# Attention steps taken in twos: where the values' product and the other work stand between the scores

## The chip, the cores and the metric

The kernel runs on one core of one Trainium2 chip. The metric is the device time of one execution in microseconds (us); lower is better. Each core has five engines with queues of their own: TensorE (PE, matrix products and transposes; its weight loads are shown as PEld), VectorE (DVE), ScalarE (ACT), GpSimd (POOL) and SyncE (SP, which issues DMAs). Each engine works through its queue in the order in which the program was written and waits at semaphores for the others. Matrix products are written to PSUM, from where DVE or ACT read them.

## The reference

`x` is (8, 512, 256) in f32. Four residual blocks follow each other, each on a layer norm of what came before:

```
x = x + attn_a(layernorm(x))     # 16 heads of 16, latent kv, RoPE, relative decay, softmax, plus a gated memory term
x = x + ffn(layernorm(x))        # 256 -> 1024 -> 256, relu
x = x + attn_b(layernorm(x))     # (q k^T * causal decay) v, no softmax
x = x + ffn(layernorm(x))        # the same weights again
```

The change concerns `attn_a`. Per head it is

```
att = softmax(q k^T / 4 + log_sparse + log(decay))    # 512 x 512 per head
out = att v + 0.2 * sigmoid(q . mean(k)) * mean(v)
```

The kernel computes the softmax as exp(0.25 * (score - row maximum)) times a table (`dec_a`, the exponential of the two added terms), and divides by the row sum after the product with v (v has a column of ones for that).

## The kernel before

Attention is cut into 32 groups (8 batch entries times 4 groups of 4 heads), each into 8 items: 4 tiles of 128 rows times 2 pairs of heads, so 256 items in all. An item passes four stations:

- *Scores s* (`score_item`, `reduce_item`): two products of 128 x 512 (32 rows of the array each) into one PSUM tile of two banks; DVE reads it once for the row maximum (`mr`).
- *Shift*: when all 8 items of a group have their maxima, one transpose (`mx`), one ACT instruction (`neg`) and a DMA put the negated maxima into spare rows of qT.
- *Transposed scores t* (`prob_item`, `soft_item`): k against q with the shift included, again two products into one PSUM tile; ACT takes the exponential into a tile `p` in SBUF; then the *decay*, two multiplications of 128 x 512 by `dec_a`, on DVE or, for every third item (`on_pool`), on POOL.
- *Values* (`pv_item`): for two items together, 4 products that add into the group's one PSUM tile `pv`, each on 32 columns of the array.

The scores s and t share the pool `ps_sc` with two buffers (four PSUM banks); `pv` has one bank, all other products (`ps_m`) three. So all eight banks are used. `p` has four buffers.

The order of all engines' instructions is written out by a planner in Python at build time. A *step* t (`step`) holds the scores of item t, the transposed scores of item t - 10 (`LAG`), and in every second step the values of items t - 12 and t - 13. Everything else (layer norms, projections, RoPE, both feed-forward blocks, `attn_b`, the output product) is cut into *units* with an assumed TensorE time and follow-up times for the other engines, in one chain for each batch entry's front part and one for its rest. The main loop (lines 898 to 945) asks for the earliest start of the next step (`step_start`) and of the best unit (`start_of`), and issues units while a credit lasts; each step adds to the credit the share of the remaining unit work that falls to one step. Below, a *run* of other work is what stands between two blocks of scores or values on TensorE. The clocks in this planner are assumptions; on the chip only queues and semaphores count.

In a step the order was: values' product first (if it has one), then s and t, then on ACT and DVE the exponential, the maximum and the decay; units follow until the next step. Items below `EARLY` = 34 use tiles of `ps_m` for t instead; they are done by step 43.

Of the kernel before, what the change touches and what calls it, by code (L numbers as in the profile page):

```python
# [35 lines left out]
def tile_kernel(  # L36
# [210 lines left out]
    NS = 8 * NI  # L247
    LAG, PVLAG = 10, 2
    PER = 8 * NG
    EARLY = PER + 2  # L250
# [249 lines left out]
    probs, pv = {}, {}  # L500

    def on_pool(n):
        return n % 2 == 0 if n < EARLY else n % 3 == 2
# [20 lines left out]
    def soft_item(n, ps):  # L524
        i, r = divmod(n, 8)
        t, pair = r // 2, 1 - r % 2
        p = at.tile([P, 2, T], F32, tag="p", bufs=4, name=f"p_{n}")
        if n < EARLY:
            for e in range(2):
                act.activation(p[:, e, :], ps[e], AF.Exp, scale=0.25)  # L530
        else:
            act.activation(p, ps[2], AF.Exp, scale=0.25)
        o = (NT - 1 - t) * P
        eng = gps if on_pool(n) else dve
        for e in range(2):
            eng.tensor_tensor(p[:, e, :], p[:, e, :], late["dec_a"][:, o : o + T], ALU.mult)
        probs[(i, t, pair)] = p

    def pv_item(n):
        i, r = divmod(n, 8)  # L540
        t = r // 2
        if t == 0:
            pv[i] = ps_pv.tile([P, T], F32, tag="pv", name=f"pv_{i}")
        g, va = i % NG, vaug[(i // NG) % 2]
        for h in range(4):
            mm(
                pv[i][h * 32 : h * 32 + 32, :], va[:, t, (NG * g + h) * 17 : (NG * g + h) * 17 + 32], probs[(i, t, h // 2)][:, h % 2, :],
                t == 0, t == NT - 1,
            )
        probs.pop((i, t, 0)), probs.pop((i, t, 1))  # L550
# [4 lines left out]
    def post_units(i):  # L555
        b, g = divmod(i, NG)
        s = {}

        def evacuate():
            num = at.tile([P, T], F32, tag="num", name=f"num_{i}")  # L560
            act.copy(num, pv[i])
            s["num"] = num

        def divide():
            if g == 0:
                a_tok[b] = at.tile([P, NT, D], F32, tag="atok", bufs=1, name=f"atok_{b}")
                aT[b] = at.tile([P, NC, T], F32, tag="aT", name=f"aT_{b}")
            ps = misc(f"num_{i}")
            for t in range(NT):
                flip(ps[:, t * P : (t + 1) * P], s["num"][:, t * P : (t + 1) * P])  # L570
            pn = ps.rearrange("p (t h d) -> p t h d", h=4, d=32)
            rd = at.tile([P, NT, 4], F32, tag="rd", name=f"rd_{i}")
            dve.reciprocal(rd, pn[:, :, :, HD])
            dve.tensor_tensor(
                a_tok[b][:, :, g * 64 : (g + 1) * 64].rearrange("p t (h d) -> p t h d", d=HD),
                pn[:, :, :, :HD], rd.unsqueeze(3).to_broadcast([P, NT, 4, HD]), ALU.mult,
            )

        def turn():
            c = g // 2  # L580
            ps = misc(f"aT_{i}")
            for t in range(NT):
                flip(ps[:, t * P : (t + 1) * P], a_tok[b][:, t, c * P : (c + 1) * P])
            act.copy(aT[b][:, c, :], ps)

        u = [Unit(evacuate, then=(("ACT", 600),))]
        u.append(Unit(divide, 520, (("DVE", 700),), after=u[-1:]))
        if g % 2:
            u.append(Unit(turn, 520, (("ACT", 600),), after=u[-1:], gives=("aT", b) if g == NG - 1 else None))
        return u  # L590
# [165 lines left out]
    clock = {"PE": 0, "DVE": 0, "ACT": 0, "POOL": 0}  # L756
    banks = deque([0, 0, 0])
# [52 lines left out]
    def values_of(t):  # L810
        n = steps[t][2]
        return n if n > 0 and n % 2 == 1 else None

    def step_start(t):

        s, ts, _ = steps[t]
        n = values_of(t)
        at_ = clock["PE"]
        if n is not None:
            at_ = max(at_, prob_at[n] - 100, prob_at[n - 1] - 100)  # L820
        own = 0
        need = (s is not None) + sum(i >= EARLY for i in ts)
        if need:
            own = sc[need - 1]
        for i in ts:
            if i < EARLY:
                own = max(own, banks[1])
            if shifted[i // 8].done is None:
                return None
            own = max(own, shifted[i // 8].done + 2300)  # L830
        return max(at_, own - (1000 if n is not None else 0))

    def step(t):
        s, ts, _ = steps[t]
        at_ = step_start(t)
        n = values_of(t)
        if n is not None:
            pv_item(n)
            at_ += 1000
            if n % 8 == 7:  # L840
                us = post_units(n // 8)
                made = Unit(None)
                made.done = at_ + 100
                us[0].after.append(made)
                posts.extend(us)
        mms, after = [], []
        if s is not None:
            ps, m = score_item(s)
            mms += m
            after.append((reduce_item, s, ps))  # L850
        for i in ts:
            ps, m = prob_item(i)
            mms += m
            after.append((soft_item, i, ps))
        for o, l, r in mms:
            mm(o, l, r)
        if mms:
            at_ += 1080
        clock["PE"] = at_
        for f, k, ps in after:  # L860
            f(k, ps)
        if s is not None:
            maxed[s] = clock["DVE"] = max(clock["DVE"], at_ + 100) + 1280
            sc.popleft()
            sc.append(maxed[s])
            if s % 8 == 7:
                posts.append(shift_unit(s // 8))
        for i in ts:
            if i < EARLY:
                for e in range(2):  # L870
                    clock["ACT"] = max(clock["ACT"], at_ + 100) + 650
                    banks.popleft()
                    banks.append(clock["ACT"])
            else:
                clock["ACT"] = max(clock["ACT"], at_ + 100) + 1090
                sc.popleft()
                sc.append(clock["ACT"])
            e = "POOL" if on_pool(i) else "DVE"
            prob_at[i] = clock[e] = max(clock[e], clock["ACT"] + 60) + (2700 if on_pool(i) else 1500)

    posts = []
    setup = [Unit(lambda: fetch(2), step=20)]
# [16 lines left out]
    while t < LAST or any(chains) or posts:  # L899
        while True:  # L900
            ready = [
                c for c in [posts] + chains
                if c and not c[0].pe and c[0].step <= t and start_of(c[0]) is not None
                and start_of(c[0]) <= clock["PE"] + 300
            ]
            if not ready:
                break
            for c in ready:
                issue(c.pop(0))
        best = None  # L910
        for rank, c in enumerate([posts] + chains):
            if not c or not c[0].pe or c[0].step > t:
                continue
            s = start_of(c[0])
            if s is None:
                continue
            key = (max(s, clock["PE"] + 50), rank)
            if best is None or key < best[0]:
                best = (key, c, s)
        s_step = step_start(t) if t < LAST else None  # L920
        if t < LAST:
            take = best is not None and (best[1] is posts or credit > 0) and (
                s_step is None or best[2] <= max(clock["PE"] + 50, s_step)
            )
            take = take or (best is not None and s_step is not None and best[2] + best[1][0].pe <= s_step)
            take = take or (best is not None and s_step is None)
            if not take and s_step is None:
                raise AssertionError("nothing to do")
        else:
            take = True  # L930
        if take and best is None:

            c = min((c for c in [posts] + chains if c and start_of(c[0]) is not None), key=lambda c: start_of(c[0]))
            clock["PE"] = max(clock["PE"], start_of(c[0]))
            issue(c.pop(0))
        elif take:
            if best[1] is not posts:
                credit -= best[1][0].pe
            issue(best[1].pop(0))
        else:  # L940
            step(t)
            t += 1
            left = sum(u.pe for c in chains for u in c) - tail_work
            share = max(0, left) / max(1, LAST - t)
            credit = min(credit, share) + share


# [107 lines left out]
```

## Time and profile before

| what | value |
|---|---|
| median of 3 runs | 1343.89 us (1341.66 to 1344.9) |
| profiled execution, its own time | 1341.52 us |
| its span, first to last instruction | 1339.7 us |
| mean granted TensorE clock | 0.978 |
| PE busy | 1256.3 us, 94% of the span |
| DVE busy | 811.0 us, 61% |
| ACT busy | 450.0 us, 34% |
| POOL busy | 405.8 us, 30% |

How to read the lines below: a line of a group names the line of the source (L69 and L205 are helpers that record every instruction), the engine, the operation, output<-inputs, shapes and count, then busy time and mean duration in ns, then the idle time of the engine before these instructions and what ended it. A line of the waits says who waited for whom, with the total in us, the count and the longest. A line of the timeline gives start, duration (both us), engine, instruction, and in brackets the idle time before it and its releaser; several records of one kind are merged into one line (xcount). Each f32 product appears as two records, a transpose as one. Matmuls are pipelined, so neighbouring ones overlap in the records; the distance from start to start is what counts.

### The profile page before, as it was taken

How to read it: one execution, taken by the hardware profiler on the slowest of the kernel's cores; microseconds unless marked ns; L12 is line 12 of the kernel's file. 1: busy time of each engine (PE TensorE's matmuls, PEld its weight loads, DVE VectorE, ACT ScalarE, POOL GpSimd, SP SyncE). 2: the span in 40 equal slices, each digit the busy share in tenths (PEclk: the TensorE clock that was granted, in tenths of full speed). 3: DMA queues.
4: the chain of work that ended last, by engine and by line, in shares of the span. 5: the costliest groups of instructions: out<-in, count | busy, mean ns of one | idle time of the engine just before them, and what ended most of it. 6: DMA issues, size and time to landing. Idle time of an engine off the chain costs nothing. (4 is left out here: it accounts for less than half of the span.)

```text
span 1339.7 us, 15533 instructions
## 1 busy us (share of the span) xinstructions
PE 1256.3 (94%) x6116; PEld 623.3 (47%) x6116; DVE 811.0 (61%) x1323; ACT 450.0 (34%) x646; POOL 405.8 (30%) x461
## 2 busy tenths in 40 slices
PE   6899888999899999999999999999999899999988
PEld 3333232534354455453443554544444445455665
DVE  4588885667656774657856666657755575343130
ACT  2044434333434334433334334333333333321201
POOL 4165542324412432215332323214321232222010
PEclk9599999989899999999999999999999999998999
DMA  5440030012000210004000310003000000000000
GB/s 133 133 80 1 1 80 1 1 26 55 1 17 1 62 19 1 1 17 80 1 1 1 74 22 1 1 9 73 1 1 5 12 1 1 1 17 1 0 16 16
DMA packets 22798, 32.34 MB, mean 24 GB/s; under 512 B 3627, under 2 KB 13228, under 8 KB 22446
## 3 DMA queue, kind: packets, MB, share of 16 engines
q1 hardware_dynamic: 22086, 31.10, 10.1%
q8 instruction: 48, 0.79, 0.3%
q10 hardware_dynamic: 640, 0.26, 0.1%
q14 instruction: 24, 0.20, 0.1%
HBM read 18.50 MB, written 12.58 MB: 23 GB/s over the span
## 5 line engine op out<-in xcount | busy, mean ns | idle before, releaser
L69 DVE TENSOR_REDUCE mr<-s 128x2 f32<-128x1024 f32 x256 | 312.8, 1222 | 251.7 <-PE t L205 237.2
L69 ACT ACTIVATE p<-t 128x1024 f32<-128x1024 f32 (+1 forms) x290 | 263.8, 924 | 519.3 <-PE t L205 476.3
L69 POOL TENSOR_TENSOR p<-p,dec_a 128x512 f32<-128x512 f32 x182 | 233.1, 1301 | 507.6 <-ACT p L69 495.0
L205 PE MATMUL s<-kT,qT 32*128 32x512 f32 x1024 | 295.3, 660 | 49.3 <-DVE mr L69 44.4
L205 PE MATMUL t<-qT,kT 32*128 32x512 f32 x1024 | 294.7, 642 | 0.3 <-ACT p L69 0.3
L69 DVE TENSOR_TENSOR p<-p,dec_a 128x512 f32<-128x512 f32 x330 | 228.9, 735 | 21.0 <-ACT p L69 20.8
L205 PE MATMUL x<-w_sb,h_x 128*128 128x256 f32 x1024 | 233.9, 384 | 0.0
L205 PEld LDWEIGHTS x<-w_sb,h_x 128*128 128x128 f32 x1024 | 190.8, 190 | 54.5 <-issue 30.1
L205 PEld LDWEIGHTS s<-kT,qT 32*128 32x128 f32 x1024 | 81.2, 189 | 221.8 <-DVE mr L69 97.5
L205 PE MATMUL pv<-p,va 128*32 128x512 f32 x1024 | 151.7, 612 | 2.9 <-DVE p L69 2.4
L69 ACT ACTIVATE h_x<-hx,vec 128x512 f32<-128x512 f32 x128 | 88.0, 687 | 151.8 <-PE hx L205 151.8
L205 PE MATMUL hx<-xT_f,w_sb 128*128 128x512 f32 x256 | 120.2, 609 | 0.7 <-ACT xT_f L69 0.7
L205 PE MATMUL hx<-xT_g,w_sb 128*128 128x512 f32 x256 | 119.3, 609 | 0.7 <-ACT xT_g L69 0.7
L69 DVE TENSOR_TENSOR x<-x,x 128x256 f32<-128x256 f32 x64 | 27.1, 423 | 148.3 <-PE x L205 148.3
L205 PEld LDWEIGHTS t<-qT,kT 32*128 32x128 f32 x1024 | 80.5, 184 | 15.9 <-ACT p L69 7.8
L205 PEld LDWEIGHTS hx<-xT_g,w_sb 128*128 128x128 f32 x256 | 46.8, 193 | 63.5 <-issue 58.1
L205 PEld LDWEIGHTS hx<-xT_f,w_sb 128*128 128x128 f32 x256 | 46.5, 194 | 58.3 <-issue 51.6
L205 PEld LDWEIGHTS pv<-p,va 128*32 128x32 f32 x1024 | 23.3, 108 | 79.3 <-issue 37.0
L69 POOL TENSOR_TENSOR x<-x,row 128x256 f32<-128x256 f32 x64 | 48.0, 770 | 32.1 <-DVE xn_f L69 21.4
L69 POOL TENSOR_TENSOR rc<-rc,rs 128x512 f32<-128x512 f32 x32 | 42.3, 1342 | 5.6 <-DVE rs L69 5.6
L205 PE MATMUL bs<-xT_r,ret 128*128 128x512 f32 (+3 forms) x128 | 38.0, 442 | 0.0
L205 PE MATMUL bo<-ret 128*128 128x256 f32 x160 | 36.6, 383 | 0.0
(130 smaller groups left out, 1020.1 us busy)
## 6 DMA issues: line engine op xcount, KB each, us to landing
dk<-rc SPq DMA_DIRECT2D x16, 256.0 KB, 2.9
kT<-dk SPq DMA_DIRECT2D x32, 128.0 KB, 3.2
dq<-rc SPq DMA_DIRECT2D x16, 256.0 KB, 2.9
qT<-dq SPq DMA_DIRECT2D x32, 128.0 KB, 3.8
out_dram<-x SPq DMA_DIRECT2D x32, 128.0 KB, 1.7
x<-in_x_dram SPq DMA_DIRECT2D x7, 512.0 KB, 3.6
w_sb<-in_w_dram SPq DMA_DIRECT2D x2, 1024.0 KB, 10.1
x<-in_x_dram SPq DMA_DIRECT2D x2, 256.0 KB
```

What stands on the lines that cost most here:

```text
L69: ins = f(*a, **k)
L205: tc.keep_in_program_order(nc.tensor.matmul(o, lhsT=l, rhs=r, start=start, stop=stop))
```

## The change

From step 44 (`EARLY` + `LAG`) to the last step that has scores of both kinds, steps go in twos (`together`). Of steps t and t + 1 the order is now: scores s and t of step t; the values' product that step t + 1 or t has to do (items t - 11 and t - 12); scores of step t + 1; then the decays of both steps' items; then one run of other work for both. The decays are taken out of `soft_item` into `decay_item`, so that on DVE they stand behind the second step's maximum instead of directly behind the own step's. Steps before 44 and after 255 keep the old order. The planner's assumed times for scores and values go from 1080 and 1000 ns to 1230 and 1200 ns, and the credit is given for two steps at a time.

```diff
             act.activation(p, ps[2], AF.Exp, scale=0.25)
+        probs[(i, t, pair)] = p
+
+    def decay_item(n):
+        i, r = divmod(n, 8)
+        t, pair = r // 2, 1 - r % 2
+        p = probs[(i, t, pair)]
         o = (NT - 1 - t) * P
         eng = gps if on_pool(n) else dve
         for e in range(2):
             eng.tensor_tensor(p[:, e, :], p[:, e, :], late["dec_a"][:, o : o + T], ALU.mult)
-        probs[(i, t, pair)] = p
...
-    def step_start(t):
+    def scores_start(t):
...
-        if n is not None:
-            pv_item(n)
-            at_ += 1000
...
         if mms:
-            at_ += 1080
+            at_ += 1230
...
+            prob_at[i] = clock["ACT"] + 60
+        return ts
+
+    def decays(ts):
+        for i in ts:
+            decay_item(i)
             e = "POOL" if on_pool(i) else "DVE"
-            prob_at[i] = clock[e] = max(clock[e], clock["ACT"] + 60) + (2700 if on_pool(i) else 1500)
+            prob_at[i] = clock[e] = max(clock[e], prob_at[i]) + (2700 if on_pool(i) else 1500)
+
+    def values(n):
+        clock["PE"] = max(clock["PE"], prob_at[n] - 100, prob_at[n - 1] - 100)
+        pv_item(n)
+        clock["PE"] += 1200
...
+    def together(t):
+
+        return [t, t + 1] if EARLY + LAG <= t < NS else [t]
+
+    def step_start(t):
+        at_ = scores_start(t)
+        n = values_of(t)
+        if at_ is not None and len(together(t)) == 1 and n is not None:
+            at_ = max(at_ - 1200, prob_at[n] - 100, prob_at[n - 1] - 100)
+        return at_
+
+    def step(t):
+        both = together(t)
+        n = values_of(both[-1])
+        if len(both) == 1:
+            if n is not None:
+                values(n)
+            decays(scores(t))
+            return
+        ts = scores(t)
+        if n is not None:
+            values(n)
+        decays(ts + scores(t + 1))
...
             step(t)
-            t += 1
+            t += len(together(t))
             left = sum(u.pe for c in chains for u in c) - tail_work
             share = max(0, left) / max(1, LAST - t)
+            share *= len(together(t)) if t < LAST else 1
             credit = min(credit, share) + share
```

More of the change, by code (lines that the diff above doesn't have):

```diff
@@ L812, in values_of, with scores @@
         return n if n > 0 and n % 2 == 1 else None
-    def step_start(t):
+    def scores_start(t):
         s, ts, _ = steps[t]
-        n = values_of(t)
         at_ = clock["PE"]
-        if n is not None:
-            at_ = max(at_, prob_at[n] - 100, prob_at[n - 1] - 100)
-        own = 0
         need = (s is not None) + sum(i >= EARLY for i in ts)
         if need:
-            own = sc[need - 1]
+            at_ = max(at_, sc[need - 1])
         for i in ts:
             if i < EARLY:
-                own = max(own, banks[1])
+                at_ = max(at_, banks[1])
             if shifted[i // 8].done is None:
                 return None
-            own = max(own, shifted[i // 8].done + 2300)
-        return max(at_, own - (1000 if n is not None else 0))
-    def step(t):
+            at_ = max(at_, shifted[i // 8].done + 2300)
+        return at_
+    def scores(t):
         s, ts, _ = steps[t]
-        at_ = step_start(t)
-        n = values_of(t)
-        if n is not None:
-            pv_item(n)
-            at_ += 1000
[L840 to L845, printed above, removed]
+        at_ = scores_start(t)
         mms, after = [], []
@@ L877, in step @@
                 sc.append(clock["ACT"])
-            e = "POOL" if on_pool(i) else "DVE"
-            prob_at[i] = clock[e] = max(clock[e], clock["ACT"] + 60) + (2700 if on_pool(i) else 1500)
+            prob_at[i] = clock["ACT"] + 60
[3 more added lines that the diff above has]
+            decay_item(i)
+            e = "POOL" if on_pool(i) else "DVE"
+            prob_at[i] = clock[e] = max(clock[e], prob_at[i]) + (2700 if on_pool(i) else 1500)
[3 more added lines that the diff above has]
+        clock["PE"] += 1200
+        if n % 8 == 7:
+            us = post_units(n // 8)
+            made = Unit(None)
+            made.done = clock["PE"] + 100
+            us[0].after.append(made)
+            posts.extend(us)
+    def together(t):
+        return [t, t + 1] if EARLY + LAG <= t < NS else [t]
+    def step_start(t):
+        at_ = scores_start(t)
+        n = values_of(t)
+        if at_ is not None and len(together(t)) == 1 and n is not None:
+            at_ = max(at_ - 1200, prob_at[n] - 100, prob_at[n - 1] - 100)
+        return at_
+    def step(t):
[10 more added lines that the diff above has]
+        decays(ts + scores(t + 1))
     posts = []
```

## The prediction

> **What bounds the kernel now.** I read the page's busy times, then the groups, the busy times by stretch, the waits, and last the timeline around single steps. On the page:
>
> ```profile
> PE 1256.3 (94%) x6116; PEld 623.3 (47%) x6116; DVE 811.0 (61%) x1323; ACT 450.0 (34%) x646; POOL 405.8 (30%) x461
> ...
> L69 DVE TENSOR_REDUCE mr<-s 128x2 f32<-128x1024 f32 x256 | 312.8, 1222 | 251.7 <-PE t L205 237.2
> ...
> L69 DVE TENSOR_TENSOR p<-p,dec_a 128x512 f32<-128x512 f32 x330 | 228.9, 735 | 21.0 <-ACT p L69 20.8
> ```
>
> TensorE (PE) is the bound at 94%; VectorE (DVE) is the next at 61%, and two thirds of its time is attention's reduces and decays. By stretch of the span (columns: stretch, length, busy time of PE, PEld, DVE, ACT, POOL, granted clock, DMA share, GB/s):
>
> ```profile
> 600.00:900.00 300.00, 290.89 (x1472) 142.00 (x1468) 199.96 (x325) 109.38 (x148) 93.33 (x106) 1.00 0.10 22
> ...
> 1160.00:1340.00 180.00, 166.96 (x650) 106.14 (x648) 46.64 (x112) 38.55 (x55) 26.24 (x37) 0.96 0.03 9
> ```
>
> The middle is TensorE work at 97%; the last 180 us hold almost no attention. The waits name what TensorE's scores wait for:
>
> ```profile
> DVE mr L69 <- PE t L205: 237.2, 148, 7.6
> ...
> PEld s L205 <- DVE mr L69: 97.5, 67, 3.2
> ...
> PE s L205 <- DVE mr L69: 44.4, 43, 2.4
> ```
>
> DVE usually waits for TensorE; but the one thing that holds TensorE is a score tile in PSUM that the max-reduce (mr) has not yet read. Two timeline readings price this. First, a run of other work between two steps, and a values' product between other work and scores:
>
> ```profile
> 401.18 3.70 PE L205 MATMUL hx<-xT_f,w_sb 128*128 128x512 f32 x8
> ...
> 404.72 0.60 PE L208 MATMUL num<-ident,num 128*128 128x128 f32 x4
> ...
> 405.25 0.70 PE L205 MATMUL s<-kT,qT 32*128 32x512 f32 x2
> ...
> 408.62 1.06 PE L205 MATMUL pv<-p,va 128*32 128x512 f32 x8
> ...
> 409.62 0.70 PE L205 MATMUL s<-kT,qT 32*128 32x512 f32 x2
> ```
>
> The eight hx records start 0.43 apart inside the block and the four num 0.11 apart: 3.44 + 0.44 = 3.88 us, but the next scores start 4.07 after the first hx. So a run of other work costs its length plus 0.19, about 0.2 us, at its two ends (first weight load not hidden, array emptied). A values' product holds TensorE 1.00 us, a step's scores 1.07 us, ends included. Second, the sequence that the change makes the rule (scores, values, scores), which the old order has now and then:
>
> ```profile
> 426.19 0.70 PE L205 MATMUL s<-kT,qT 32*128 32x512 f32 x2
> ...
> 427.26 1.07 PE L205 MATMUL pv<-p,va 128*32 128x512 f32 x8
> ...
> 427.36 1.23 DVE L69 TENSOR_REDUCE mr<-s 128x2 f32<-128x1024 f32 x1 [0.39 <-PE t L205]
> ...
> 428.64 0.70 PE L205 MATMUL s<-kT,qT 32*128 32x512 f32 x2 [0.32 <-DVE mr L69]
> 429.82 1.23 DVE L69 TENSOR_REDUCE mr<-s 128x2 f32<-128x1024 f32 x1
> ```
>
> The pool of score tiles has two buffers, and a step takes both, one for s and one for t. So the next s waits for the last s's reduce: 1.17 us from scores to the reduce's start, 1.23 for it, 0.05 back: 2.45 us from scores to scores, where TensorE needs only 1.07 + 1.00 = 2.07. That is 0.38 us of standstill with DVE free at once, and more if DVE is late.
>
> **What the Trainium skill says.** "TensorEngine Tiling (Array Packing)", section Key Properties: "Mode switching requires drain". Scores (32-row tiles), values (32-column tiles) and the rest (whole array) are three modes, and the 0.2 us above agrees. The same page, PSUM Bottleneck: tiling speeds up TensorE but not PSUM evacuation; here 1.07 us of scores leave a 1.23 us reduce. "VectorE: DVE Perf Modes", The perf-mode tier table: tensor_reduce has only the 1x rate, so the reduce isn't shortened by a quieter neighbourhood; the trace shows 1193 to 1228 ns over all 256. "TensorE: Matmul & The Clock Gate", Step-by-step: matmuls stay in program order; so behind the waiting scores stands everything else on TensorE, the run of other work too, and the waits above agree.
>
> **The change part by part.** Counts come from the order of instructions in the two builds, from step 44's scores on.
>
> *Removed.* Between scores 44 and scores 255 there were 178 runs of other work, now 107: 71 x 0.2 = 14.2 us saved. The matmuls themselves are the same ones; nothing is dropped.
>
> *Moved, the first cost.* Scores-values-scores stood 18 times in the old order; now 105 pairs have it. Each pays 0.38 us at least: 40 us. In the old trace all 18 waited, 0.39 at the least and 17.7 us together. No work can hide it: only the values' product stands between, and both buffers are in use.
>
> *Moved, the second cost.* In the old order a wait for DVE hurts only where steps stand close. Now the reduce of a pair's first step always has a pair waiting behind it, so each lateness of DVE is paid by TensorE. Both decays (two instructions, 1.29 us each on DVE; every third one is on POOL) are queued on DVE after the pair's second reduce, ahead of the next pair's first, with the layer norms, evacuations and RoPE products of the run. With R the run's length on TensorE (0.2 included) and D the DVE work between the two reduces, the next first reduce is late by about D - R. I added up R from block lengths and D from the groups' durations for all 105 pairs. In 65 pairs R is 3 us or more (mean 7.5, mean D 4.2): late by 7 us in all, 0.1 each, and the old trace agrees, where reduces after such long runs started 0.03 to 0.08 late in the mean. In 29 pairs R is 1.4 to 3 (mean 2.2 against D 3.05): 27 us. In 11 it is under 1.4 (0.6 against 2.7): 23 us. Sum 57 us.
>
> *Moved, the third cost.* A pair whose run is under 1.4 us also waits at its own start for the previous pair's second reduce (2.45 after its scores): 8.6 us over 11 pairs.
>
> *What goes.* The old order's own waits of this kind: between scores 44 and 255 TensorE stood 69.6 us in waits. 22.7 were scores directly after scores (14 times), 17.7 scores-values-scores, 7.7 scores after a run, 6.4 scores after values that followed a run: 54.5 us. The other 15 are runs waiting for layer norms, values for decays, and t for the shift's DMA. Adding up the old order in the same way gives 51 us for those 54.5, so the way of counting holds there.
>
> *Other edits.* Values now have the run and one scores block between the decays and themselves. On POOL a decay takes 2.5 us (two of 1.3); where R is under 2.6 the product may wait, but that wait runs alongside the late reduce of the same pair: 0 to 5 us, I take 2. The four p buffers are each freed by the previous pair's values: nothing. The shift for group 6 now stands right ahead of its first t, and neg, DMA issue and landing cost some 3 us once; two such places existed before, so 0. Longer runs hold more dependent units back to back (old waits of that kind 7.9 us): -3 to +10, I take +2. No SP or POOL DMA gets more bytes or issues. The work after the last values' product is equal (123.0 against 123.5 us).
>
> *Sum.* 40 + 57 + 8.6 - 54.5 = +51; -14.2 for runs; +4 for the rest: +41 us. Profiled execution 1341.5 (span 1339.7 and 1.8 around it) + 41 = 1382.5; the median 1343.9 is 2.4 above that execution, so 1385 for a median.
>
> **Rivals.**
> (a) *The tight stretches are cheaper than D - R.* If half of the lateness in short runs (25 of 50 us) is overlapped, say because layer norm work on DVE slips past unnoticed, +16: 1360. For it: D takes each instruction at its mean and puts every one ahead of the reduce. Against: the count reproduces the old waits.
> (b) *The planner's misjudgement spreads.* Its slots for pairs assume 1230 and 1200 ns, and no reduce wait inside a pair; dependent units in a run then stand closer to their sources, POOL decays hold values, evacuations make long runs' reduces late by 0.3 (65 x 0.2 = 13 more). With the upper ends above +65: 1408.
> (c) *Faster.* The 14.2 us are sure, and the old 54.5 us of waits could vanish because pairs leave DVE a whole run to catch up. If first reduces are never late: 40 + 8.6 - 54.5 - 14.2 = -20, 1324. It decides from the point where the lateness totals under 20 us, a third of my 57. Against: in the 40 short pairs DVE's own work is 2 x 1.22 + 3.0 = 5.4 us, TensorE's 1.07 + 1.00 + 1.07 + 1.8 = 4.9; DVE is the bound there whatever the order, and the pair adds a hole of 1.2 us between its two reduces, which the old order filled with a decay.
> (d) *It does not do what it says*: excluded, the order shows the 105 pairs.
>
> **How the numbers follow.** The main case, 1365 to 1400, 0.64; (a), 1349 to 1365, 0.14; (b), over 1400, 0.13; (c) 0.06; within 0.3% (4 us, about what a measurement of this kernel can tell) 0.03. Predicted 1385. The range 1355 to 1403 leaves out about 2 in 10. Slower 0.91, same 0.03, faster 0.06.
>
> **What would show it.** In the new trace: scores to scores within a pair never under 2.45 us, with DVE mr as releaser some 105 times; the waits of PE s and PEld s on DVE mr up from 44.4 and 97.5; PE busy falling from 94% to some 91%; reduces late after short runs, punctual after long ones; some 70 fewer mode changes. Wrong it would be if pairs stood 2.07 apart, or if the short runs showed reduces that start 1.17 after their scores.

## The result, and the profile after

The changed kernel takes 1399.4 us (median of 4, 1398.0 to 1401.0) where the kernel before takes 1343.1; the ratio is 1.043, with an interval of 1.041 to 1.046. It is 56 us slower. The forecast was 1385, slower by 41, with a range of 1355 to 1403.

The page of the changed kernel, in the lines that answer to those of before (granted clock 0.979 against 0.978):

```profile
span 1398.7 us, 15523 instructions
...
PE 1268.1 (91%) x6116; PEld 630.2 (45%) x6116; DVE 832.2 (60%) x1323; ACT 451.2 (32%) x646; POOL 442.0 (32%) x461
...
L69 DVE TENSOR_REDUCE mr<-s 128x2 f32<-128x1024 f32 x256 | 312.4, 1221 | 276.1 <-PE t L205 264.6
...
L69 POOL TENSOR_TENSOR p<-p,dec_a 128x512 f32<-128x512 f32 x182 | 267.1, 1487 | 514.9 <-ACT p L69 448.6
...
L69 DVE TENSOR_TENSOR p<-p,dec_a 128x512 f32<-128x512 f32 x330 | 261.4, 842 | 28.9 <-ACT p L69 28.9
```

POOL's line in the kernel before, which was not shown yet:

```profile
L69 POOL TENSOR_TENSOR p<-p,dec_a 128x512 f32<-128x512 f32 x182 | 233.1, 1301 | 507.6 <-ACT p L69 495.0
```

TensorE falls from 94% to 91%, as forecast. The reduces are as long as before. But the decays, the same instructions on the same data, got longer on both engines: 735 to 842 ns on DVE, 1301 to 1487 ns on POOL. The forecast had no such term.

By stretch (stretch, length, busy time of PE, PEld, DVE, ACT, POOL, granted clock, DMA share, GB/s), and the waits:

```profile
600.00:900.00 300.00, 278.17 (x1391) 135.46 (x1392) 197.73 (x313) 105.46 (x141) 100.24 (x102) 0.99 0.10 22
```

```profile
PEld s L205 <- DVE mr L69: 187.9, 127, 3.2
...
PE s L205 <- DVE mr L69: 78.5, 106, 2.3
...
PEld pv L205 <- POOL p L69: 37.1, 34, 1.5
...
PEld pv L205 <- DVE p L69: 35.8, 46, 3.9
```

In the middle TensorE is busy for 278 of 300 us instead of 291. The matmul wait of scores s on the maximum mr now occurs 106 times instead of 43: 95 of these stand at a pair's second scores, 11 elsewhere, mostly at a pair's start. (There are also 106 pairs, but that the two numbers are equal is chance. The lines of PEld are idle time of the weight loads, which is not by itself time lost.)

Where the time went, from the starts of all TensorE records (in us; a run of other work is counted with its length and 0.2 for its ends, scores with 1.07, values with 1.00, and what is over is counted as wait; the spans are those of the profiled executions):

| stretch | before | after | change |
|---|---|---|---|
| up to scores 44 | 158.4 | 157.4 | -1.0 |
| scores 44 to scores 255 | 997.2 | 1040.3 | +43.1 |
| of which waits | 69 | 146 | +77 |
| of which fewer ends of runs (179 runs, now 104) | | | -15.0 |
| of which other work that now stands later | | | -18.9 |
| scores 255 to the last values' product | 39.7 | 61.4 | +21.7 |
| the rest | 144.4 | 139.7 | -4.7 |
| span | 1339.7 | 1398.7 | +59.0 |

The 18.9 us of work come back in the third stretch, so the sum is +77 - 15, with -3 in the other places. The new waits: 107.6 at scores-values-scores (17.7 before), 12.0 at values inside a pair, 16 at the start of a pair. Below, the *lateness* of a reduce is the time from its scores to its start, less the 1.17 us that it takes at best; that of the pairs' first reduces adds up to 76 us.

One place in the changed kernel's timeline shows all of it:

```profile
526.23 1.19 DVE L69 TENSOR_REDUCE mr<-s 128x2 f32<-128x1024 f32 x1
...
527.48 0.70 PE L205 MATMUL s<-kT,qT 32*128 32x512 f32 x2 [1.52 <-DVE mr L69]
...
528.65 1.23 DVE L69 TENSOR_REDUCE mr<-s 128x2 f32<-128x1024 f32 x1 [1.23 <-PE t L205]
...
529.79 2.36 DVE L69 TENSOR_TENSOR p<-p,dec_a 128x512 f32<-128x512 f32 x2
529.81 3.46 POOL L69 TENSOR_TENSOR p<-p,dec_a 128x512 f32<-128x512 f32 x2 [2.38 <-ACT p L69]
...
532.19 0.70 PE L205 MATMUL s<-kT,qT 32*128 32x512 f32 x2
...
533.26 1.13 PE L205 MATMUL pv<-p,va 128*32 128x512 f32 x8
...
534.82 1.22 DVE L69 TENSOR_REDUCE mr<-s 128x2 f32<-128x1024 f32 x1
536.09 0.70 PE L205 MATMUL s<-kT,qT 32*128 32x512 f32 x2 [1.70 <-DVE mr L69]
```

The first pair's second scores (527.48) wait for a late reduce. Between that pair's two reduces DVE stands idle for 1.23 us: the hole. Then the pair's two decays begin at the same moment on two engines, and take 2.36 and 3.46 us instead of 1.29 and 2.5. The next pair's first reduce could start 1.17 us after 532.19, at 533.36; it starts at 534.82, behind the decay and the run's own DVE work, and TensorE stands 1.70 us.

### The profile page after: what moved, and what is told of

The parts are those of the page before. It is cut to its first block, busy times and chain, and to the rows that moved or that the text cites. A ratio compares the mean times of both kernels' runs of the same rounds, so it can differ in the third digit from the quotient of the medians.

```text
span 1398.7 us, 15523 instructions
## 1 busy us (share of the span) xinstructions
PE 1268.1 (91%) x6116; PEld 630.2 (45%) x6116; DVE 832.2 (60%) x1323; ACT 451.2 (32%) x646; POOL 442.0 (32%) x461
## 4 chain that ended last, share of the span: by engine, by line
PE 64%; DVE 27%; issue 3%; POOL 3%; ACT 2%; DMA 1%; SPq 0%; POOLq 0%; DVEq 0%; ACTq 0%
PE x L205 15%; PE hx L205 15%; PE s L205 14%; DVE mr L69 11%; DVE p L69 7%; PE wo L205 3%; PE pv L205 3%; PE bo L205 2%; PE t L205 2%; POOL p L69 2%; PE b L205 1%; ACT p L69 1%; PE bv L205 1%; PE q L205 1%; DVE ret L69 1%
## 5 line engine op out<-in xcount | busy, mean ns | idle before, releaser
L69 POOL TENSOR_TENSOR p<-p,dec_a 128x512 f32<-128x512 f32 x182 | 267.1, 1487 | 514.9 <-ACT p L69 448.6
L205 PE MATMUL t<-qT,kT 32*128 32x512 f32 x1024 | 298.3, 652 | 1.0 <-DMA qT<-neg 0.7
L69 DVE TENSOR_TENSOR p<-p,dec_a 128x512 f32<-128x512 f32 x330 | 261.4, 842 | 28.9 <-ACT p L69 28.9
L205 PE MATMUL x<-w_sb,h_x 128*128 128x256 f32 x1024 | 230.8, 382 | 0.0
L205 PE MATMUL pv<-p,va 128*32 128x512 f32 x1024 | 169.3, 612 | 18.8 <-DVE p L69 9.4
L205 PE MATMUL hx<-xT_f,w_sb 128*128 128x512 f32 x256 | 115.1, 595 | 0.0
L205 PEld LDWEIGHTS pv<-p,va 128*32 128x32 f32 x1024 | 26.2, 108 | 138.1 <-issue 42.5
L69 POOL TENSOR_TENSOR rc<-rc,rs 128x512 f32<-128x512 f32 x32 | 43.7, 1385 | 13.8 <-DVE rs L69 13.8
```

Source lines behind the costliest of these rows:

```text
L69: ins = f(*a, **k)
L205: tc.keep_in_program_order(nc.tensor.matmul(o, lhsT=l, rhs=r, start=start, stop=stop))
```

## The experiments

The theory after the first look has three parts: each pair pays 0.38 us for the score buffers (A); reduces that are late because both decays and the run's work are queued ahead of them are paid by TensorE, as in the forecast (B); and the decays of DVE and POOL, now often at the same time, slow each other down and make the reduces later still (C). The rivals are that the cut of the runs or the planner's numbers place units badly, and that only the buffers count. Times below are medians of 4 runs (20 for the last kernel); the kernel before, run beside them each time, had 1341.6 to 1342.6.

**The first decay back at its own step.**

```diff
-    def decays(ts):
+    def decays(ts, placed=()):
         for i in ts:
-            decay_item(i)
+            if i not in placed:
+                decay_item(i)
...
         ts = scores(t)
+        for i in ts:
+            decay_item(i)
         if n is not None:
             values(n)
-        decays(ts + scores(t + 1))
+        decays(ts + scores(t + 1), ts)
```

The planner's books stay as they were, so TensorE's order does too.

> The changed kernel, but the first step's decay stands directly behind its own exponential and maximum again, ahead of the values' product; TensorE's order and everything else are those of the changed kernel (1399). Theory (reduces of first steps are late because both decays are queued ahead of them): two pairs in three have a first-step decay on DVE, 1.29 us, which now fills the hole between the pair's two reduces; in the 39 pairs with a run under 3 us that takes 0.86 us each off the lateness, 33 us, and a little more from fewer collisions with POOL: 1355 to 1370. The wait of 0.38 us in each pair stays, so it does not come back to 1343. Rival 1 (lateness comes from the run's own layer norms and evacuations, not from the decays): 1390 to 1399. Rival 2 (only the two score buffers count): no change, 1399.

Measured 1359.0, ratio to the kernel before 1.013 (1.011 to 1.014). Lateness of first reduces fell from 76 us to 33. Rivals 1 and 2 of this run fall: where the decays stand is worth 40 us. How much of this is the queue (B) and how much the collisions (C), this run doesn't say: DVE's decays beside one of POOL's fell from 100 records to 35 too. The same place in the timeline of this kernel:

```profile
510.98 1.28 DVE L69 TENSOR_TENSOR p<-p,dec_a 128x512 f32<-128x512 f32 x2
511.12 0.70 PE L205 MATMUL s<-kT,qT 32*128 32x512 f32 x2 [1.52 <-DVE mr L69]
...
512.29 1.23 DVE L69 TENSOR_REDUCE mr<-s 128x2 f32<-128x1024 f32 x1
...
513.45 2.50 POOL L69 TENSOR_TENSOR p<-p,dec_a 128x512 f32<-128x512 f32 x2 [2.38 <-ACT p L69]
...
517.49 1.22 DVE L69 TENSOR_REDUCE mr<-s 128x2 f32<-128x1024 f32 x1
...
518.76 0.70 PE L205 MATMUL s<-kT,qT 32*128 32x512 f32 x2 [0.80 <-DVE mr L69]
```

DVE's decay sits in the hole between the two reduces and delays the second one by nothing (512.29 is 1.17 after the scores). POOL's decay then runs alone and takes 2.50 us instead of 3.46. The first pair waits 1.52 us as before, behind layer norm work on DVE; the second 0.80 instead of 1.70.

**The maximum over a quarter of the columns, in pairs and in single steps.**

```diff
-            mrow[i % 2][:, 2 * pair : 2 * pair + 2, t], ps, AX.X, ALU.max
+            mrow[i % 2][:, 2 * pair : 2 * pair + 2, t], ps if n < EARLY + LAG else ps[:, :, :P], AX.X, ALU.max
```

> The changed kernel with the maximum taken over the first 128 of the 512 columns only, from item 44 on: three quarters of the reduce's computation are left out, so the shift isn't the true maximum; TensorE's order is unchanged. A reduce should take some 0.4 us (128x256 read from PSUM by DVE take 0.42). Theory (the pair's price is the wait for the reduce): the s buffer is free 1.64 us after the scores, under the 2.07 that TensorE needs; then the t buffer decides (exponential, 2.30), so a pair stands 0.2 us instead of 0.38, and the second reduce ends 0.8 us earlier, so lateness falls by 35 to 45: some 1335 to 1345 us, and the distance to the old order with the same cut falls from 56 to 10 to 25 us. Rival (the price lies in how the runs of other work are cut and where units stand): the distance stays over 40.

> The kernel before with the same cut: maximum over the first 128 of 512 columns from item 44 on, three quarters of the reduce left out. The old order's waits for the reduce (54 us between scores 44 and 255) shrink to those for the exponential: 14 places of scores on scores wait 1.23 instead of 1.6, 18 of scores-values-scores 0.2 instead of 1.0, the rest nearly nothing: 20 to 30 us less, 1313 to 1325.

Measured 1331.8 in pairs and 1316.8 in single steps, so the distance is 15 us instead of 56, as theory A and B together say, and the rival (over 40 whatever the reduce) falls. One pair of the first kernel:

```profile
611.96 0.70 PE L205 MATMUL s<-kT,qT 32*128 32x512 f32 x2
...
613.39 0.41 DVE L69 TENSOR_REDUCE mr<-s 128x2 f32<-128x256 f32 x1
614.02 0.70 PE L205 MATMUL s<-kT,qT 32*128 32x512 f32 x2
614.27 0.70 PE L205 MATMUL t<-qT,kT 32*128 32x512 f32 x2
```

The reduce takes 0.42 us; scores to scores within a pair have a median of 2.07 us, TensorE's own time, instead of 2.84. The t products start 0.25 us behind the s products, where they otherwise follow at once: the t buffer costs 19.5 us of waits inside the second scores (0.2 each), as expected. Two sizes were missed: the pairs came out 3 us below their range, and their lateness fell by 30 us (76 to 46), not by 35 to 45.

**POOL's decays left out, in pairs.**

```diff
         eng = gps if on_pool(n) else dve
+        if n >= EARLY and on_pool(n):
+            return
```

> The changed kernel with the decays of POOL left out from item 34 on (every third item isn't multiplied by the decay table); DVE's and TensorE's orders are unchanged. In the changed kernel's trace 100 of the 330 records of DVE's decays ran beside a POOL instruction and took 1.21 us instead of 0.68 (36 of 330 before). Theory (decays on both engines at the same time slow each other down, and this makes first reduces later than D - R said): all DVE decays at 0.68, DVE's decays 35 us shorter in all, lateness of first reduces from 76 to 50 to 60, and the values' waits for POOL vanish: 1365 to 1380. Rival (the longer records are the profile's rough spans or are hidden): lateness stays above 70; only the values' waits go, 1390 to 1397.

Measured 1362.3. The records of DVE's decays are 698 ns in the mean instead of 842, lateness is 47 us instead of 76 (the forecast's own count, without collisions, was 57), and values never wait for POOL. The time and the lateness both lie 3 us below what was expected. The direction is that of C, and the rival falls; but this run also takes away the values' waits and work of POOL, and so the next one separates them better.

**POOL takes a pair's first item.**

```diff
-        eng = gps if on_pool(n) else dve
+        on = on_pool(n) if n < EARLY else n % 6 in (2, 4)
+        eng = gps if on else dve
```

> The changed kernel with POOL taking the same number of decays from item 34 on, but always a pair's first item (items 2 and 4 of every six instead of 2 and 5); nothing is left out, TensorE's order is the same. In the changed kernel a second item's decay on POOL starts at the very time at which DVE, done with the second maximum, starts the first item's; a first item's decay on POOL is nearly done by then. Theory (both engines' decays at once slow each other, and that is what made first reduces later than counted): DVE's records beside POOL fall from 100 to 30 or 40, its mean decay record from 842 to about 740 ns, lateness of first reduces from 76 to 50 to 60, and the values wait less for POOL: 1370 to 1382. Rival (the lateness is DVE's queue length alone, which is the same here): 1393 to 1399.

Measured 1372.5, 27 us less with every instruction kept and TensorE's order unchanged. Its page:

```profile
L69 POOL TENSOR_TENSOR p<-p,dec_a 128x512 f32<-128x512 f32 x182 | 232.4, 1298 | 438.1 <-ACT p L69 438.1
...
L69 DVE TENSOR_TENSOR p<-p,dec_a 128x512 f32<-128x512 f32 x330 | 228.8, 744 | 30.2 <-ACT p L69 30.2
```

Both engines' decays have their old lengths again (842 to 744, 1487 to 1298 ns). 35 records of DVE's stand beside a multiplication of POOL for over 0.3 us instead of 100, and lateness is 50 us. The same place in its timeline:

```profile
511.56 2.49 POOL L69 TENSOR_TENSOR p<-p,dec_a 128x512 f32<-128x512 f32 x2
511.64 0.70 PE L205 MATMUL s<-kT,qT 32*128 32x512 f32 x2 [1.52 <-DVE mr L69]
...
513.96 1.28 DVE L69 TENSOR_TENSOR p<-p,dec_a 128x512 f32<-128x512 f32 x2
...
517.61 1.22 DVE L69 TENSOR_REDUCE mr<-s 128x2 f32<-128x1024 f32 x1
518.88 0.70 PE L205 MATMUL s<-kT,qT 32*128 32x512 f32 x2 [0.40 <-DVE mr L69]
```

POOL starts early, DVE's decay follows when POOL is nearly done, and the second pair waits 0.40: nothing but the price of the buffers. The rival, queue length alone, falls. Beside the first run this divides its 40 us: about 27 go with the collisions, about 13 with the place of DVE's decays in the queue. Some of the 27 can be values that wait less, since POOL's decays are also done sooner here.

**The late decay in single steps.**

```diff
+        probs[(i, t, pair)] = p
+        if n >= EARLY and n % 2 == 0:
+            return
+        for m in ([n - 1, n] if n > EARLY else [n]):
+            decay_item(m)
+
+    def decay_item(n):
...
-        probs[(i, t, pair)] = p
```

> The kernel before with the one part of the change that the decays are: single steps in the old order on TensorE, but the decay of an even step stands behind the next step's maximum, together with that step's decay. With the kernel before, the pairs with the decay at its own step (1359) and the changed kernel (1399) this fills the square of both parts. Theory (lateness of a reduce is paid only where scores wait right behind it, which is everywhere in pairs and in some 32 places of the old order): 1345 to 1358, so the moved decay costs 40 in pairs and under 15 in single steps. Rival (late decays cost by themselves, through the values that wait for p): 1375 to 1385, the same 40 in both.

Measured 1367.8, between the theory (up to 1358) and the rival (from 1375): late decays cost 26 us in single steps and 40 in pairs. The waits in the old order rose from 70 to 95. This expectation was wrong in size. The trace shows a term that it left out: the decays collide here as they do in pairs. 115 of DVE's decay records stand beside a multiplication of POOL (36 before), and they take longer:

```profile
L69 POOL TENSOR_TENSOR p<-p,dec_a 128x512 f32<-128x512 f32 x182 | 271.3, 1510 | 420.1 <-ACT p L69 390.3
...
L69 DVE TENSOR_TENSOR p<-p,dec_a 128x512 f32<-128x512 f32 x330 | 273.2, 879 | 18.3 <-ACT p L69 18.3
```

So the collisions come from where the decay stands, not from the pairs. In pairs the delay is paid more fully: when the decays move from their own step to the late place, the lateness of all reduces between scores 44 and 255 rises by 41 us and the waits by 46; in single steps the lateness rises by 34 and the waits by 26.

**The planner's numbers alone.**

```diff
-        return [t, t + 1] if EARLY + LAG <= t < NS else [t]
+        return [t]
```

> The changed code with the pairs switched off: every step is single again (values, then scores, decays at once), but the planner keeps its new assumed times (1230 and 1200 ns) and its new rule for a step's start. TensorE's order differs from that before only in where some units stand (179 runs instead of 178, 19 places of scores-values-scores instead of 18, 12 of scores on scores instead of 14). Theory (the pairs are the cause, not the planner's numbers): 1336 to 1350, nothing of the 56. Rival (the new times scatter the units badly): over 1360.

Measured 1355.9, ratio 1.012 (1.008 to 1.016): 14 us slower, where nothing was expected. The assumed times of 1230 and 1200 ns and the new rule for a step's start move some units. Of the 13.7 us in the profiled executions 8.9 lie between scores 44 and 255 (waits rose from 70 to 75 us there, and some other work moved in), the rest in small parts in the other stretches; no one place stands out. The pairs with the old times were not tried, so how much of the changed kernel's 56 us comes from its numbers stays open.

**The planner told of the wait.** `clock["PE"] += 1580` in place of 1200 after a values' product, and `at_ - 1580` in place of `at_ - 1200` in `step_start`, which only the steps that stay single use.

> The changed kernel, but the planner assumes 1580 ns for a values' product instead of 1200, so that a pair's scores-to-scores time in its books is 2.81 us, as the trace shows (median 2.84); everything else is as changed. Single steps with the planner's other new times had cost 14 us more than expected, so its numbers matter. Theory (the pair's price is on the chip, in the two buffers and DVE's queue): 1385 to 1405. Rival (a good part of the 56 us is units put in bad places because the planner doesn't know of the wait): 1360 to 1380.

Measured 1408.0, 3 us above the expectation. Books that agree with the chip on a pair's length don't help: lateness is still 69 us. The rival falls as far as this one assumed time goes; other times may place the units better.

**Both losses taken away.** Quarter maximum and first decay at its own step, both edits from above.

> The changed kernel with both of its losses taken away: maximum over 128 of the 512 columns from item 44 on (three quarters of the reduce left out) and the first step's decay back behind its own maximum. Theory (14 us saved at the ends of the runs are real and the rest was the reduce's wait and the lateness): the late reduces of the pairs with the quarter maximum (46 us) fall to some 20, so 1332 becomes 1305 to 1315, under the old order with the same cut (1317). Rival (the ends of the runs save nothing, or the pairs have a further cost): 1318 to 1330.

Measured 1326.0, in the rival's range, so the expectation failed. The trace shows where: first reduces are late by 30 us instead of 46, but second ones by 19 instead of 2. One pair, whose first scores start at 497.87:

```profile
499.15 1.02 ACT L69 ACTIVATE p<-t 128x1024 f32<-128x1024 f32 x1 [3.26 <-issue]
...
499.99 0.70 PE L205 MATMUL s<-kT,qT 32*128 32x512 f32 x2
500.21 1.29 DVE L69 TENSOR_TENSOR p<-p,dec_a 128x512 f32<-128x512 f32 x2 [0.27 <-ACT p L69]
...
501.42 0.42 DVE L69 TENSOR_REDUCE mr<-s 128x2 f32<-128x256 f32 x1
```

The decay waits for its exponential, which comes no sooner because the reduce is short: it starts about 2.3 us after the first scores, as in the kernel with the whole maximum, and takes 1.29. But the second scores come 0.38 us sooner, so the second reduce, which could start at 501.16, starts at 501.42. The waits of t for the exponential's buffer (21 us) had been left in as well. The ends of the runs are saved here too (104 runs), so "they save nothing" isn't shown; what is shown is that the pair order with two buffers loses elsewhere what it saves.

**Both repairs that leave nothing out, and the second one in single steps.**

> The changed kernel with both repairs that leave nothing out: the first step's decay at its own step, and POOL taking the first items (2 and 4 of six). Theory (what then remains is the pairs' fixed price, 106 waits of 0.38 us less 14 us for the ends of the runs, with the old order's waits in tight places exchanged for a like lateness): only one pair in three has a first decay on DVE, which stands in the hole; lateness 25 to 33 and 1350 to 1360, so still slower than the kernel before. Rival (lateness was all of it, and without it the pairs are worth their 14 us): under 1340.

> The kernel before with the same other choice of POOL's items (2 and 4 of every six from item 34 on), single steps, nothing left out. Only 36 of its 330 decay records stood beside POOL, and few reduces have scores waiting behind them: 1337 to 1346, no difference that can be told. Rival (the choice of items is an improvement by itself, so that it explains the 27 us that it gave in pairs): 1315 to 1330.

In pairs, with the decay at its own step and POOL on the first items: 1357.9, no better than the decay alone (1359.0). Each repair removes the same collisions; lateness is 33 us in both. This is the lowest that pairs reached with nothing left out, 1.4% over the kernel before (ratio 1.014, 1.009 to 1.018), and the rival, under 1340, falls. Counted as in the table, waits are about 31 us longer here than in the kernel before and the ends of runs 15 shorter, which agrees with the 15.5 us measured. But the planner's numbers alone cost single steps 14 us, so whether pairs with better placed units would still be slower is not shown. In single steps the choice of POOL's items gives 1336.0 against 1342.4, ratio 0.996 (0.995 to 0.998), just below the expected range and 0.4% faster than the kernel before, with all work kept. It has as many records beside POOL as before (35 to 36), so collisions don't explain its 6 us. In the trace the gain lies between scores 44 and 255 (991.0 against 997.2 us), in shorter waits; why they are shorter is open.

## Why the prediction was right, and which of its terms were off

*The sign and the mechanism* held. Within a pair no scores came closer than 2.45 us in the changed kernel; with the reduce cut to 0.42 us the closest were 2.07 apart. Rival (c), faster if the lateness stays under 20 us, failed by its own point: the lateness was 76. The size was less sure: 1399.4 lies at the upper edge of the main case (1365 to 1400).

*Fewer ends of runs*: 14.2 us forecast, from 178 runs that become 107, with 105 pairs. The order of TensorE's instructions in the two kernels has 179 runs, 104 runs and 106 pairs, so 75 x 0.2 = 15.0. No run isolates it, but between other work and scores the new trace leaves nearly no unexplained rest at 0.2 (median under 0.01 us).

*The fixed wait*: 0.38 us for each pair, 40 us. It stands: in each of the 106 pairs the scores are at least 2.45 us apart.

*The lateness*, D - R, is the term that was mis-sized: 57 us forecast, 76 measured. By class: runs under 1.4 us 23 forecast and 22 measured; 1.4 to 3 us 27 and 36; longer 7 and 18. What was wrong is the duration in D, "1.29 us each on DVE", taken from a mean in which few decays had POOL beside them. In the new trace 100 records beside POOL's multiplications take 1.21 us each instead of 0.68. The two runs that keep DVE's queue but remove the collisions bring the lateness to 47 and 50, so the rest of D - R was counted 7 to 10 us too high. It was too high in the shortest runs: with POOL on the first items the three classes have 14, 26 and 10 us. That the shortest class came out at its 23 was luck, an overcount and the missing collisions together.

*Waits at a pair's start* were 16 us instead of 8.6. *Values waiting for decays* were 12 us instead of 2; POOL's decay was taken at 2.5 us, where colliding ones take 3.4. But the forecast's reason for the small term was right: these waits run alongside the late reduce of the same pair. Both waits of the pairs come to 107.6 + 12.0 = 119.6 us, only some 3 more than 106 x 0.38 + 76.

*The rest*: the old order's other waits, which the forecast let stand at 15 us and 2 more, came to about 10. The end of the kernel, forecast as equal, was 4.7 us shorter, which no run explains. The planner's own numbers, which rival (b) named as assumptions, cost 14 us by themselves in single steps; the forecast's main case had nothing for them, and no run shows what they cost in pairs. In the profiled executions the distance is 59 us where 41 were forecast: lateness +19, values on top of it +1 to +2, a pair's start +7, other waits -7, ends of runs -1 and the other stretches -3 make some 17 of these 18 us. The medians are 56 us apart.

## What to carry to other kernels

Before two users of a double buffer are put close together, compare what stands between them with the time until the buffer comes back: here 2.07 us of TensorE's work against 2.45 us, so that saving 75 switches of 0.2 us cost a wait of 0.38 us in each of 106 pairs. Then look at what the engine that frees the buffer has queued ahead of it: an instruction that was free in the shadow of a long run is on the path once somebody waits behind it. And when instructions are regrouped, ask which engines now work at the same time; a mean duration from the old order holds for the old neighbours only.

## What the runs showed of the hardware

Multiplications on DVE and POOL that both read and write SBUF stretch each other: 0.68 us alone and 1.21 together on DVE, 1.27 and 1.71 on POOL, in the changed kernel's trace. The Trainium skill, "SBUF — State Buffer", section SBUF: two separate sides, says that a DVE operation with two SBUF inputs and a GpSimd operation that reads SBUF share a pair of ports under a lock: whichever starts first has it for its whole instruction, and the other waits. The records of the place shown above, one by one:

```profile
529.79 0.68 DVE L69 TENSOR_TENSOR p<-p,dec_a 128x512 f32<-128x512 f32 x1
529.81 1.79 POOL L69 TENSOR_TENSOR p<-p,dec_a 128x512 f32<-128x512 f32 x1 [2.38 <-ACT p L69]
...
530.39 1.76 DVE L69 TENSOR_TENSOR p<-p,dec_a 128x512 f32<-128x512 f32 x1
...
531.56 1.71 POOL L69 TENSOR_TENSOR p<-p,dec_a 128x512 f32<-128x512 f32 x1
```

They end in turn, at 530.47, 531.60, 532.15 and 533.27. The first is as short as one alone. Each of the others ends 1.13, 0.55 and 1.12 us after the one before it, 0.13 to 0.15 less than its length alone, so both engines together need 3.48 us where one after the other they would need 1.29 + 2.5 = 3.8. The trace thus agrees with taking turns, apart from the small overlap, and it shows the waiting as busy time. It agrees too that a reduce from PSUM, which has no two SBUF inputs, isn't touched: 1.22 us alone, 1.22 beside POOL.
